# Mixture-of-experts stage of a four-layer graph network: units of 196 rows from a list made on the chip in place of 64 blocks of 784 rows

## The chip, the cores and the metric

The kernel runs on one core of a Trainium2 chip. The metric is the device time of one execution in microseconds (us). The kernel before has a median of 7043.7 us in 14 runs (7037.86 to 7055.6).

## The reference, cut to what matters

A graph of 12500 nodes with 128 features and 200000 edges goes through four layers, each followed by a residual and a layernorm: a weighted mean over neighbours, the layer below, and two more sums over neighbours. The change lies in the second layer: a graph convolution, then 64 experts of which every node uses two, then a batchnorm.

```python
new_feats = gcn_conv(feats, edge_src, edge_dst, W_conv, b_conv)
scores = new_feats @ gate_W + gate_b
topv, topi = top_k(scores, 2);  gw = softmax(topv)
# pos: how many earlier (node, choice) pairs took the same expert
C = 2 * ceil(2 * 12500 / 64)                     # 782
slot = eid * C + where(pos < C, pos, 0)
buf = zeros((64 * C, 128)).at[slot].add(where(pos < C, x_rep, 0))
hact = gelu(einsum('ecd,edh->ech', buf, W1) + b1)        # hidden width 256, exact gelu
y = einsum('ech,ehd->ecd', hact, W2) + b2
core = sum over the two choices of gw * y[slot] * (pos < C)
out = batchnorm(new_feats + core)
```

25000 pairs are spread over 64 experts, 391 on average, while 782 places are reserved for each.

## The kernel before

The engines are PE (TensorE; its loads of the stationary operand are listed as PEld), DVE (VectorE), ACT (ScalarE), POOL (GpSimd) and SP, which only issues transfers. SP, ACT and POOL each issue DMAs from an in-order queue of their own; an instruction that waits holds back all behind it on its engine. Around the change a scheduler orders the instructions of each engine from the program's order and the buffers that pools hold; nothing is placed by hand there. A pool with `bufs=2` lets the next loop step start before the last is done with its tile, and a tile in memory that an earlier stage held waits for that stage's last use.

The stages that matter, with line numbers of the profile:

- **First layer (to about 2140 us).** Edge messages are gathered and scattered by POOL (scatter at L751). Between, SP loads a window for each of 391 edge blocks, with a register load (L657) and a load at the register's address (L661). Among these loads stand the writes that fill `buf` with zeros: `buf` lies in DRAM with 64 x 784 rows for the experts and spare rows behind them for pairs without a place. Each write is 458 KB, one after every sixth window until 56 are done (L668 to L670).
- **Routing (3926 to 4235 us).** For groups of seven tiles of 128 nodes: convolution weights, scores, two maxima, softmax gates, and the place of each pair in its expert. `run` holds the number of pairs of each expert so far (L1363, L1364), `come` the row to fetch later (L1381). POOL scatters each tile's rows twice into `buf` (L1388).
- **Experts (4235 to 4823 us, L1398 to L1442).** `b1` is loaded and transposed once. The loop runs over 64 experts with SL = 784 rows each, as 7 tiles of TT = 112. Per expert SP loads `w1` (L1411) and `w2` (L1413), 128 KB each; ACT loads `b2` (L1415) and 392 KB of rows `xt` (L1417). PE transposes seven tiles (L1422), DVE copies them out (L1423, L1424). Four hidden groups follow, two halves of the hidden width by two halves of the rows: matmuls into 392 columns (L1429) and a gelu with `b1` on ACT (L1431). Then come 14 output products of 112 rows (L1436), one addition of `b2` on DVE (L1439), and a store of 392 KB into `ybuf` by SP (L1440). An f32 matmul of the program is several PE instructions in the trace: 256 hidden products are 512, 896 output products are 1792.
- **Counts.** Beside experts and combine the kernel makes tables for later edge sums: 98 counts (`band_counts`). One count is a set of comparisons on DVE (`fs` L1073, `fd` L1075), 17 PE instructions into four banks (L1089), four casts on ACT (L1091) and a store of 512 KB by SP (L1093). EXB = 48 of them are spread over the expert loop, the other 50 over the combine loop.
- **Combine (4823 to 5116 us).** For each of 98 node tiles and both choices POOL gathers 128 rows of `ybuf` (L1476) and DVE adds them with the gate (L1479); sums for the batchnorm follow every fourth tile.

The lines that set sizes and the fill:

```python
TT = 112
NTT = 7
SL = TT * NTT
DUMP = NE * SL
...
EXB = 48
...
                    if i % 6 == 5 and fill:
                        r = fill.pop(0)
                        Y.dma_start(bz[:, r:r + step], zero)
```

Of the kernel before, what the change touches and what calls it, by code (L numbers as in the profile page):

```python
# [10 lines left out]
F32 = mybir.dt.float32  # L11
# [3 lines left out]
I32 = mybir.dt.int32  # L15
AF = mybir.ActivationFunctionType
OP = mybir.AluOpType
AX = mybir.AxisListType
PSUM = bass.MemoryType.PSUM
DRAM = bass.MemoryType.DRAM  # L20

P = 128
N = 12500
D = 128
# [12 lines left out]
NE = 64  # L37
TOPK = 2
HID = 256
CAP = 2 * -(-N * TOPK // NE)  # L40
TT = 112
NTT = 7
SL = TT * NTT
DUMP = NE * SL
EPS = 1e-15
LN_EPS = 1e-5
# [18 lines left out]
LW = 96  # L65
WC = 16
BANK = 512
EXB = 48
MAXC = 256


# [67 lines left out]
def gnn_kernel(ctx: ExitStack, tc: tile.TileContext, a, out: bass.AP):  # L139
    nc = tc.nc  # L140
    V, S, G, T, Y = nc.vector, nc.scalar, nc.gpsimd, nc.tensor, nc.sync

    const = ctx.enter_context(tc.tile_pool(name="const", bufs=1))
    dram = ctx.enter_context(tc.tile_pool(name="dram", bufs=1, space=DRAM))
# [6 lines left out]
    iota = const.tile([P, P], F32, name="iota")  # L151
# [3 lines left out]
    ident = const.tile([P, P], F32, name="ident")  # L155
# [5 lines left out]
    ones = const.tile([P, P], F32, name="ones")  # L161
# [40 lines left out]
    off_d = [dram.tile([NK, P], I32, name=f"off_d{i}") for i in (0, 1)]  # L202
    counts = [dram.tile([NT, P, b.width], BF16, name=f"counts{i}") for i, b in enumerate(BANDS)]
    buf = dram.tile([DUMP + NT * TOPK * P, D], F32, name="buf")
    ybuf = dram.tile([DUMP, D], F32, name="ybuf")


    def newton_sqrt(pool, v, tag):
# [22 lines left out]
    def bc(v, n):  # L231
        return v[:, :, None].to_broadcast([P, v.shape[1], n])
# [256 lines left out]
    def spread_edges(bad):  # L489


        ET = mybir.EngineType
        NR = 6
        TAIL = NB - (NBK - 1) * P
        with tc.tile_pool(name="sc", bufs=1) as pc, tc.tile_pool(name="scp", bufs=1, space=PSUM) as pps:
            rows = pc.tile([P, NR, 4, W3], BF16, name="rows")
# [29 lines left out]
            if True:  # L526
# [3 lines left out]
                with tc.tile_pool(name="rf", bufs=1) as pa, tc.tile_pool(name="rfp", bufs=2, space=PSUM) as tp_:  # L530
# [105 lines left out]
            with tc.tile_pool(name="sb", bufs=4) as lp, tc.tile_pool(name="sw", bufs=3) as wk, \  # L636
                    tc.tile_pool(name="sg", bufs=2, space=PSUM) as gp:
                step = 7 * D
                zero = pc.tile([P, step], F32, name="zero")
                V.memset(zero, 0.0)  # L640
                bz = buf[0:DUMP, :].rearrange("(p r) f -> p (r f)", p=P)
                empty = list(range(NT - 1))
                fill = list(range(0, DUMP // P * D, step))
                one_ps = pps.tile([NT + 1, EB], F32, name="one_ps")
                V.memset(one_ps, 1.0)
                d_ps = pps.tile([P, NT], F32, name="d_ps")
                start = pc.tile([NT + 1, 1], F32, name="start")
# [3 lines left out]
                st = {"end": start}  # L651
                rb, win, hot, rank, low, gps = {}, {}, {}, {}, {}, {}

                def fetch(i):
                    rb[i] = lp.tile([P, 2 * EB], BF16, name="rb")
                    Y.dma_start(rb[i], rows_d[i].partition_broadcast(P))
                    _, at = nc.values_load_multi_w_load_instructions(  # L657
                        first_r[0:1, i:i + 1], engines=[ET.SP], min_val=0, max_val=NP - 1,
                        skip_runtime_bounds_check_because="clamped to the last node on the chip")
                    win[i] = lp.tile([P, 3, D + 1], BF16, name="win")  # L660
                    Y.dma_start(win[i].rearrange("p k f -> p (k f)"), table0[ds(at[0], P), :])  # L661
                    if 4 <= i < MID - 20 and empty:

                        for _ in range(-(-NT // (MID - 24))):
                            cl = clear(empty.pop(0), SURE, RB)
                            tc.declare_no_dep(cl.ins, group="spread", reason="rows that no edge has yet")
                            tc.add_to_no_dep_group("blank", cl.ins)
                    if i % 6 == 5 and fill:  # L668
                        r = fill.pop(0)
                        Y.dma_start(bz[:, r:r + step], zero)  # L670

                def places(i):
                    t = wk.tile([P, EB], BF16, name="hot")
# [36 lines left out]
                with tc.manual_schedule(engines={ET.DVE, ET.PE, ET.Activation}):  # L710
                    for i in range(-2, NB):
# [590 lines left out]
    with tc.tile_pool(name="moe", bufs=1) as pm:  # L1302
# [92 lines left out]
        at_.close()  # L1395


        with tc.tile_pool(name="ex", bufs=2) as wk, tc.tile_pool(name="exb", bufs=2, space=PSUM) as pb, \  # L1398
                tc.tile_pool(name="exh", bufs=2, space=PSUM) as ph_, tc.tile_pool(name="exc", bufs=1) as pc, \
                band_pools("x") as band:  # L1400
            b1n = pc.tile([NE, HID], F32, name="b1n")
            Y.dma_start(b1n, a["L1_gnn_b1"])
            b1T = pc.tile([P, 2, NE], F32, name="b1T")
            for j in range(2):
                pb1 = ph_.tile([P, 512], F32, name="ph")
                T.transpose(pb1[:, 0:NE], b1n[:, j * P:(j + 1) * P], ident[:NE, :NE])
                V.tensor_copy(b1T[:, j, :], pb1[:, 0:NE])
            HALF = SL // 2
            for e in range(NE):
                w1 = wk.tile([P, HID], F32, name="w1")  # L1410
                Y.dma_start(w1, a["L1_gnn_W1"][e])  # L1411
                w2 = wk.tile([P, 2, D], F32, name="w2")
                Y.dma_start(w2, a["L1_gnn_W2"][e].rearrange("(j p) d -> p j d", p=P))  # L1413
                b2 = wk.tile([TT, D], F32, name="b2")
                S.dma_start(b2, a["L1_gnn_b2"][e].partition_broadcast(TT))  # L1415
                xt = wk.tile([TT, NTT, D], F32, name="xt")
                S.dma_start(xt, buf[e * SL:(e + 1) * SL, :].rearrange("(i p) f -> p i f", p=TT))  # L1417
                px = pb.tile([P, 1024], F32, name="pw")
                bT = wk.tile([P, SL], F32, name="bT")
                for i in range(NTT):  # L1420
                    o = i * TT if i < 4 else 512 + (i - 4) * TT
                    T.transpose(px[:, o:o + TT], xt[:, i, :], ident[:TT, :TT])  # L1422
                V.tensor_copy(bT[:, 0:4 * TT], px[:, 0:4 * TT])  # L1423
                V.tensor_copy(bT[:, 4 * TT:SL], px[:, 512:512 + 3 * TT])  # L1424
                hT = wk.tile([P, 2, SL], F32, name="hT")
                for j in range(2):
                    for q in range(2):
                        ph = ph_.tile([P, 512], F32, name="ph")
                        T.matmul(ph[:, 0:HALF], w1[:, j * P:(j + 1) * P], bT[:, q * HALF:(q + 1) * HALF],  # L1429
                                 start=True, stop=True)  # L1430
                        S.activation(hT[:, j, q * HALF:(q + 1) * HALF], ph[:, 0:HALF], AF.Gelu,  # L1431
                                     bias=b1T[:, j, e:e + 1])
                py = pb.tile([P, 8, D], F32, name="pw")
                for i in range(NTT):
                    for j in range(2):
                        T.matmul(py[:TT, i, :], hT[:, j, i * TT:(i + 1) * TT], w2[:, j, :],  # L1436
                                 start=(j == 0), stop=(j == 1))
                ye = wk.tile([TT, NTT, D], F32, name="ye")
                V.tensor_tensor(ye, py[:TT, 0:NTT, :], b2[:, None, :].to_broadcast([TT, NTT, D]), OP.add)  # L1439
                Y.dma_start(ybuf[e * SL:(e + 1) * SL, :].rearrange("(i p) f -> p i f", p=TT), ye)  # L1440
                for s in range(EXB * e // NE, EXB * (e + 1) // NE):
                    band_counts(band, s)  # L1442


# [25 lines left out]
        with tc.tile_pool(name="cm", bufs=12) as wk, tc.tile_pool(name="cs", bufs=2) as sw, band_pools("c") as band:  # L1470
            for t in range(NT):
                for s in range(EXB + (NT - EXB) * t // NT, EXB + (NT - EXB) * (t + 1) // NT):
                    band_counts(band, s)
                for k in range(TOPK):
                    yk = wk.tile([P, D], F32, name="yk")
                    G.indirect_dma_start(out=yk, out_offset=None, in_=ybuf[:, :],  # L1476
                                         in_offset=bass.IndirectOffsetOnAxis(ap=come[:, t, k:k + 1], axis=0))
                    o = A3[:, t, 0:D]
                    V.scalar_tensor_tensor(o, yk, gates[:, t, k:k + 1], o, op0=OP.mult, op1=OP.add)  # L1479
                stats(sw, t)  # L1480
# [130 lines left out]
```

## Time and profile before

| what | value |
|---|---|
| median of 14 runs | 7043.7 us |
| profiled execution, its own time | 7042.59 us |
| its span in the trace | 7040.8 us |
| mean granted TensorE clock | 0.933 |
| instructions | 106434 |
| busy share of the span: PE, DVE, ACT, POOL | 73%, 61%, 29%, 55% |
| DMA | 1375.96 MB, mean 195 GB/s |
| routing, experts, combine | 309, 588, 293 us |

Times in the trace are microseconds from the start of the span. The span is 1.8 us shorter than the profiled execution's own time. A line of the timeline gives start, duration, engine, source line, operation, output and inputs by the program's names, and in brackets how long the engine had stood idle and what released it. A line of a group gives the number of instructions, the total busy time and the mean in nanoseconds of one, and the idle time before them with its releasers. The clock column is the share of full TensorE speed that was granted.

### The profile page before, as it was taken

Reading aid. Unit: us, or ns where it says so; the run is one execution under the profiler, and the core shown is the slowest. Engines: PE = TensorE matmul, PEld = TensorE weight load, DVE = VectorE, ACT = ScalarE, POOL = GpSimd, SP = SyncE. Lnnn points to the kernel's source line nnn. Section 1 sums busy time; section 2 is a strip of 40 time slices with the busy share of each in tenths; the row PEclk is TensorE's granted clock in tenths of the full one; section 3 lists DMA queues with packets and bytes.
Section 4 is the critical chain, followed back from the end, with each engine's and each line's share of the span. In section 5 each row is a group of like instructions: output and inputs, shape, how many; then the busy total and the mean of one; then the engine's idle time right before and its main releaser. Section 6 shows DMA issues by size and latency. Waiting matters only on the chain. (4 is left out here: it accounts for less than half of the span.)

```text
span 7040.8 us, 106434 instructions
## 1 busy us (share of the span) xinstructions
PE 5132.4 (73%) x32620; PEld 3139.8 (45%) x33009; DVE 4267.9 (61%) x11730; ACT 2018.9 (29%) x4176; POOL 3889.1 (55%) x3917
## 2 busy tenths in 40 slices
PE   0666666666664566699998548998809998699995
PEld 0444444444442233355554336664305444355544
DVE  6887777777775778766675574557991223411115
ACT  3343333333331223333332113444440001100003
POOL 0677777777773000577777570004707776477760
PEclk9999999999999888899999569999959999799998
DMA  9976555555557999355554115554458889688862
GB/s 247 272 220 204 159 152 153 152 152 151 151 153 231 324 318 303 124 165 165 166 166 151 47 56 159 166 164 137 142 156 277 288 291 294 205 293 290 282 230 63
DMA packets 1046137, 1375.96 MB, mean 195 GB/s; under 512 B 106732, under 2 KB 848744, under 8 KB 1045566
## 3 DMA queue, kind: packets, MB, share of 16 engines
q1 hardware_dynamic: 803208, 960.67, 44.4%
q0 software_dynamic: 181312, 376.38, 17.1%
q10 hardware_dynamic: 61046, 31.77, 1.6%
q8 instruction: 301, 4.93, 0.3%
q14 instruction: 270, 2.21, 0.1%
HBM read 911.40 MB, written 457.00 MB: 194 GB/s over the span
## 5 line engine op out<-in xcount | busy, mean ns | idle before, releaser
L1134 POOL DMA_INDIRECT fg<-table,e_row x1952 | 1956.9, 1003 | 1519.4 <-SPq L1023 676.8
L1125 PE MATMUL dense<-fc_a,fc_x 128*128 128x512 bf16 x7422 | 1874.8, 381 | 215.2 <-DMA fc_x<-table 205.3
L751 POOL DMA_INDIRECT msg<-rows,to x1564 | 1509.8, 965 | 656.8 <-issue 393.5
L1125 PEld LDWEIGHTS <-fc_x 128*128 128x128 bf16 x7644 | 678.5, 98 | 795.6 <-issue 194.6
L1227 DVE TENSOR_TENSOR AT<-AT,fps 128x512 f32 x122 | 83.9, 688 | 1490.4 <-PE fps L1151 1448.3
L1089 PE MATMUL fb_ps<-fd,fs 128*128 128x512 bf16 (+7 forms) x3942 | 877.1, 340 | 75.0 <-DMA fg<-table,e_row 31.5
L701 PE MATMUL g_ps<-rows,minus 128*128 128x258 bf16 x1564 | 462.7, 399 | 637.5 <-ACT rows L734 603.2
L734 ACT CAST rows<-g_ps 128x516 bf16<-128x516 f32 x1173 | 698.7, 596 | 642.0 <-PE g_ps L701 296.6
L695 PE MATMUL g_ps<-win,hot 128*128 128x129 bf16 x4692 | 650.6, 311 | 215.7 <-DMA win<-table 116.4
L1075 DVE TENSOR_SCALAR fd<-iota_h,hd 128x128 bf16<-128x128 f16 (+6 forms) x1563 | 786.6, 508 | 0.0
L1151 PEld LDWEIGHTS <-fg 128*128 128x128 bf16 x5856 | 464.1, 98 | 525.9 <-DMA fg<-table,e_row 97.9
L695 PEld LDWEIGHTS <-hot 128*128 128x128 bf16 x4692 | 535.3, 143 | 294.8 <-issue 195.2
L1151 PE MATMUL fps<-fh,fg 128*128 128x96 bf16 x5856 | 580.9, 208 | 95.8 <-DMA fg<-table,e_row 75.3
L868 PE MATMUL ce_sum<-ce_r,ce_s 128*128 128x390 bf16 x1764 | 380.5, 382 | 275.5 <-DVE ce_s L865 267.8
L1476 POOL DMA_INDIRECT yk<-ybuf,come x196 | 219.5, 1120 | 652.1 <-DMA counts<-bc_a 592.6
L1089 PEld LDWEIGHTS <-fs 128*128 128x128 bf16 x4108 | 377.1, 98 | 372.2 <-issue 110.0
L701 PEld LDWEIGHTS <-minus 128*128 128x128 bf16 x1564 | 199.7, 128 | 765.1 <-issue 765.0
L1091 ACT CAST fc_a<-fb_ps 128x512 bf16<-128x512 f32 x588 | 344.1, 585 | 634.0 <-PE fb_ps L1089 634.0
L679 DVE TENSOR_TENSOR_SCAN run_ps<-one_ps,run_ps,bin 99x512 f32<-99x512 f32 x390 | 505.4, 1296 | 13.8
L1073 DVE TENSOR_SCALAR fs<-iota_b,hs 128x128 bf16<-128x128 bf16 x1563 | 410.3, 265 | 39.4 <-PE fb_ps L1089 35.6
L868 PEld LDWEIGHTS <-ce_s 128*128 128x128 bf16 x1764 | 190.3, 112 | 465.8 <-DVE ce_s L865 259.6
L1091 ACT CAST bc_a<-fb_ps 128x512 bf16<-128x512 f32 x392 | 227.6, 584 | 448.5 <-PE fb_ps L1089 361.8
(382 smaller groups left out, 6245.3 us busy)
## 6 DMA issues: line engine op xcount, KB each, us to landing
ce_r<-msg SPq DMA_DIRECT2D x98, 1782.0 KB
fc_a<-counts SPq DMA_DIRECT2D x196, 768.0 KB
fc_a<-counts SPq DMA_DIRECT2D x196, 512.0 KB
rb<-rows_d SPq DMA_DIRECT2D x391, 256.0 KB
counts<-fc_a SPq DMA_DIRECT2D x98, 768.0 KB
counts<-bc_a SPq DMA_DIRECT2D x98, 512.0 KB
fc_x<-table SPq DMA_DIRECT2D x490, 96.0 KB
msg<-blank SPq DMA_DIRECT2D x99, 396.0 KB
```

The costliest lines, as they stand in the source:

```text
L679: V.tensor_tensor_scan(c, one_ps, b, st["end"], OP.mult, OP.add)
L695: T.matmul(gps[i][:, q, 0:D + 1], hot[i][:, q * P:(q + 1) * P], win[i][:, k, :], start=(q == 2 * half and k == 0), stop=False)
L701: T.matmul(gps[i][:, 2 * h:2 * h + 2, 0:D + 1], minus, r[:, 2 * h:2 * h + 2, k * W0:k * W0 + D + 1], start=False, stop=True, skip_group_ch ...
L734: S.copy(r[:, :, k * W0:k * W0 + D + 1], gt)
L751: sc = G.indirect_dma_start(out=msg[:, :], out_offset=bass.IndirectOffsetOnAxis(ap=to[:, q:q + 1], axis=0), in_=r[:, q, :], in_offset=None)
L868: T.matmul(ps, sel[:, j, :], r[:, j, 0:3 * W0], start=(j == 0), stop=(j == RB - 1))
L1075: V.tensor_scalar(col[:, 0:hi - lo], iota_h[:, 0:hi - lo], hd[self.i][:, s, q:q + 1], None, op0=OP.is_equal)
L1089: T.matmul(ps[:, lo - c0:hi - c0], self.sel[s, j], self.col[s, j][:, lo - w[j][0]:hi - w[j][0]], start=(j == first), stop=(j == js[-1]))
L1091: S.copy(out[:, c0:c1], ps)
L1125: T.matmul(dense[n], xr[s][:, k, :], cnt[s][:, n * BANK:(n + 1) * BANK], start=(s == 0 and k == 0), stop=(s == NT - 1 and k == 2))
L1134: G.indirect_dma_start(out=g[q][:, i].rearrange("p k f -> p (k f)"), out_offset=None, in_=table[:, :], in_offset=bass.IndirectOffsetOnAxis ...
L1151: T.matmul(ps[:, ds(at[0], LW)], g[i // 4][:, i % 4, k, :], hot[i // 4][:, i % 4, :], start=False, stop=(i == WC - 1 and k == 2))
```

## The change

Rows are computed in units of UR = 196 rows (two tiles of TT = 98), four units to an expert, so the place of each expert stays at 784 rows. A static loop runs over NU = 191 units, the most that 25000 pairs can need. Which expert and which rows a unit has is read from a list made on the chip: from the number of pairs of each expert, the number of units it needs, running sums of these, and for each unit the expert, the offset of its `b2`, the unit of rows to read and the unit of rows to write. The list goes through DRAM into one partition. Units past the last needed one read rows of the last expert and write to spare rows behind `ybuf`.

Each unit reads its entries into registers: two on SP, two on ACT, one on DVE. `w1`, `w2`, `xt` and the store use them as addresses, gelu's bias and the addition of `b2` as offsets. `b2` of all experts is loaded once, copied to 98 partitions. Weights are loaded for each unit, with three buffers in place of two. `ybuf`, parts of which are no longer written, is filled with zeros like `buf`, a write after every third window until 112 are done. EXB becomes 60, so 38 counts are left for the combine. The pools in PSUM have two buffers each for transposes, hidden and output tiles.

```diff
-TT = 112
-NTT = 7
-SL = TT * NTT
+TT = 98
+UR = 2 * TT
+UE = 4
+SL = UR * UE
+NU = (N * TOPK + NE * (UR - 1)) // UR
 DUMP = NE * SL
...
-EXB = 48
+EXB = 60
...
-    ybuf = dram.tile([DUMP, D], F32, name="ybuf")
+    ybuf = dram.tile([DUMP + NU * UR, D], F32, name="ybuf")
+    unit_d = dram.tile([8, P], I32, name="unit_d")
...
-                    if i % 6 == 5 and fill:
-                        r = fill.pop(0)
-                        Y.dma_start(bz[:, r:r + step], zero)
+                    if i % 3 == 2 and fill:
+                        Y.dma_start(fill.pop(0), zero)
...
+            b2r = pc.tile([TT, NE * D], F32, name="b2r")
+            Y.dma_start(b2r, a["L1_gnn_b2"].rearrange("e d -> (e d)").partition_broadcast(TT))
             b1n = pc.tile([NE, HID], F32, name="b1n")
             Y.dma_start(b1n, a["L1_gnn_b1"])
...
+                T.matmul(t_ps[:, 0, 0:NE], ones, run, start=True, stop=True)
+                n = pu.tile([P, NE], F32, name="un_n")
+                V.tensor_scalar_min(n, t_ps[:, 0, 0:NE], float(CAP))
+                u = pu.tile([P, NE], F32, name="un_u")
+                V.tensor_scalar(u, n, 0.0, None, op0=OP.is_gt)
+                for k in range(1, UE):
+                    V.scalar_tensor_tensor(u, n, float(k * UR), u, op0=OP.is_gt, op1=OP.add)
+                end = pu.tile([P, NE], F32, name="un_end")
+                V.tensor_tensor_scan(end, ones[:, 0:NE], u, 0.0, OP.mult, OP.add)
...
+                T.transpose(w_ps[0:8, 0, 0:P], what.rearrange("p w k -> p (w k)"), ident)
+                w_i = pu.tile([8, P], I32, name="un_i")
+                V.tensor_copy(w_i, w_ps[0:8, 0, 0:P])
+                Y.dma_start(unit_d, w_i)
+                Y.dma_start(unit_r, unit_d.rearrange("w p -> (w p)").rearrange("(o c) -> o c", o=1))
...
+            def number(kind, j, engine, most):
+                _, v = nc.values_load_multi_w_load_instructions(
+                    unit_r[0:1, kind * 2 * P + j:kind * 2 * P + j + 1], engines=[engine], min_val=0, max_val=most,
...
+                return v[0]
...
-            for e in range(NE):
+            for j in range(NU):
+                e = number(0, j, ET.SP, NE - 1)
+                w1 = wk.tile([P, 1, HID], F32, name="w1")
+                Y.dma_start(w1, w1s[:, ds(e, 1), :])
+                w2 = wk.tile([P, 1, 2, D], F32, name="w2")
+                Y.dma_start(w2, w2s[:, ds(e, 1), :, :])
+                xt = wk.tile([TT, 1, 2, D], F32, name="xt")
+                S.dma_start(xt, rows_in[:, ds(number(2, j, ET.Activation, NE * UE - 1), 1), :, :])
+                px = pb.tile([P, UR], F32, name="px")
+                for i in range(2):
+                    T.transpose(px[:, i * TT:(i + 1) * TT], xt[:, 0, i, :], ident[:TT, :TT])
+                bT = wk.tile([P, UR], F32, name="bT")
+                V.tensor_copy(bT, px)
+                ph = pb.tile([P, 2, UR], F32, name="ph")
+                hT = wk.tile([P, 2, UR], F32, name="hT")
+                e1 = number(0, j, ET.Activation, NE - 1)
+                for k in range(2):
+                    T.matmul(ph[:, k, :], w1[:, 0, k * P:(k + 1) * P], bT, start=True, stop=True)
+                    S.activation(hT[:, k, :], ph[:, k, :], AF.Gelu, bias=b1T[:, k, ds(e1, 1)])
+                py = pb.tile([P, 2, D], F32, name="py")
+                for i in range(2):
+                    for k in range(2):
+                        T.matmul(py[:TT, i, :], hT[:, k, i * TT:(i + 1) * TT], w2[:, 0, k, :],
+                                 start=(k == 0), stop=(k == 1))
+                ye = wk.tile([TT, 1, 2, D], F32, name="ye")
+                e2 = number(1, j, ET.DVE, (NE - 1) * D)
+                for i in range(2):
+                    V.tensor_tensor(ye[:, 0, i, :], py[:TT, i, :], b2r[:, ds(e2, D)], OP.add)
+                st = Y.dma_start(rows_out[:, ds(number(3, j, ET.SP, NE * UE + NU - 1), 1), :, :], ye)
...
+                for s in range(EXB * j // NU, EXB * (j + 1) // NU):
                     band_counts(band, s)
...
-                    G.indirect_dma_start(out=yk, out_offset=None, in_=ybuf[:, :],
+                    G.indirect_dma_start(out=yk, out_offset=None, in_=ybuf[0:DUMP, :],
```

More of the change, by code (lines that the diff above doesn't have):

```diff
@@ L640, in spread_edges @@
                 V.memset(zero, 0.0)
-                bz = buf[0:DUMP, :].rearrange("(p r) f -> p (r f)", p=P)
+                blanks = [b[0:DUMP, :].rearrange("(p r) f -> p (r f)", p=P) for b in (buf, ybuf)]
                 empty = list(range(NT - 1))
-                fill = list(range(0, DUMP // P * D, step))
+                fill = [b[:, r:r + step] for b in blanks for r in range(0, DUMP // P * D, step)]
                 one_ps = pps.tile([NT + 1, EB], F32, name="one_ps")
@@ L1395, in gnn_kernel @@
         at_.close()
-        with tc.tile_pool(name="ex", bufs=2) as wk, tc.tile_pool(name="exb", bufs=2, space=PSUM) as pb, \
-                tc.tile_pool(name="exh", bufs=2, space=PSUM) as ph_, tc.tile_pool(name="exc", bufs=1) as pc, \
-                band_pools("x") as band:
+        ET = mybir.EngineType
+        with tc.tile_pool(name="ex", bufs=3) as wk, tc.tile_pool(name="exp", bufs=2, space=PSUM) as pb, \
+                tc.tile_pool(name="exc", bufs=1) as pc, band_pools("x") as band:
+            unit_r = pc.tile([1, 8 * P], I32, name="unit_r")
+            b1T = pc.tile([P, 2, NE], F32, name="b1T")
+            b2r = pc.tile([TT, NE * D], F32, name="b2r")
+            Y.dma_start(b2r, a["L1_gnn_b2"].rearrange("e d -> (e d)").partition_broadcast(TT))
@@ L1401, in gnn_kernel @@
             b1n = pc.tile([NE, HID], F32, name="b1n")
             Y.dma_start(b1n, a["L1_gnn_b1"])
-            b1T = pc.tile([P, 2, NE], F32, name="b1T")
             for j in range(2):
[L1405 to L1408, printed above, removed]
-            for e in range(NE):
[L1410 to L1441, printed above, removed]
@@ new lines, in gnn_kernel @@
+                pb1 = pb.tile([P, 2, UR], F32, name="ph")
+                T.transpose(pb1[:, 0, 0:NE], b1n[:, j * P:(j + 1) * P], ident[:NE, :NE])
+                V.tensor_copy(b1T[:, j, :], pb1[:, 0, 0:NE])
+            with tc.tile_pool(name="un", bufs=1) as pu:
+                t_ps = pb.tile([P, 2, UR], F32, name="ph")
+                T.matmul(t_ps[:, 0, 0:NE], ones, run, start=True, stop=True)
[7 more added lines that the diff above has]
+                V.tensor_tensor_scan(end, ones[:, 0:NE], u, 0.0, OP.mult, OP.add)
+                shift = pu.tile([P, NE], F32, name="un_shift")
+                V.tensor_sub(shift, u, end)
+                V.scalar_tensor_tensor(shift, iota[:, 0:NE], float(UE), shift, op0=OP.mult, op1=OP.add)
+                ji = pu.tile([P, 2], I32, name="un_ji")
+                G.iota(ji, pattern=[[P, 2]], base=0, channel_multiplier=1)
+                jf = pu.tile([P, 2], F32, name="un_j")
+                V.tensor_copy(jf, ji)
+                pick = pu.tile([P, 2, NE], F32, name="un_pick")
+                V.tensor_tensor(pick, end[:, None, :].to_broadcast([P, 2, NE]), bc(jf, NE), OP.is_le)
+                what = pu.tile([P, 4, 2], F32, name="un_what")
+                V.tensor_reduce(what[:, 0, :], pick, AX.X, OP.add)
+                V.tensor_scalar_min(what[:, 0, :], what[:, 0, :], float(NE - 1))
+                V.tensor_scalar_mul(what[:, 1, :], what[:, 0, :], float(D))
+                V.tensor_tensor(pick, iota[:, None, 0:NE].to_broadcast([P, 2, NE]), bc(what[:, 0, :], NE), OP.is_equal)
+                V.tensor_tensor(pick, pick, shift[:, None, :].to_broadcast([P, 2, NE]), OP.mult)
+                V.tensor_reduce(what[:, 2, :], pick, AX.X, OP.add)
+                V.tensor_add(what[:, 2, :], what[:, 2, :], jf)
+                V.tensor_scalar_min(what[:, 2, :], what[:, 2, :], float(NE * UE - 1))
+                over = pu.tile([P, 2], F32, name="un_over")
+                V.tensor_tensor(over, jf, end[:, NE - 1:NE].to_broadcast([P, 2]), OP.is_ge)
+                V.tensor_scalar_add(what[:, 3, :], jf, float(NE * UE))
+                V.tensor_sub(what[:, 3, :], what[:, 3, :], what[:, 2, :])
+                V.tensor_mul(what[:, 3, :], what[:, 3, :], over)
+                V.tensor_add(what[:, 3, :], what[:, 3, :], what[:, 2, :])
+                w_ps = pb.tile([P, 2, UR], F32, name="ph")
+                T.transpose(w_ps[0:8, 0, 0:P], what.rearrange("p w k -> p (w k)"), ident)
[3 more added lines that the diff above has]
+                Y.dma_start(unit_r, unit_d.rearrange("w p -> (w p)").rearrange("(o c) -> o c", o=1))
@@ new lines, in number @@
+            def number(kind, j, engine, most):
+                _, v = nc.values_load_multi_w_load_instructions(
+                    unit_r[0:1, kind * 2 * P + j:kind * 2 * P + j + 1], engines=[engine], min_val=0, max_val=most,
+                    skip_runtime_bounds_check_because="clamped to the last expert's units on the chip")
+                return v[0]
+            rows_in = buf[0:DUMP, :].rearrange("(u i p) f -> p u i f", i=2, p=TT)
+            rows_out = ybuf.rearrange("(u i p) f -> p u i f", i=2, p=TT)
@@ new lines, in gnn_kernel @@
+            w1s = a["L1_gnn_W1"].rearrange("e p h -> p e h")
+            w2s = a["L1_gnn_W2"].rearrange("e (j p) d -> p e j d", p=P)
+            for j in range(NU):
[27 more added lines that the diff above has]
+                st = Y.dma_start(rows_out[:, ds(number(3, j, ET.SP, NE * UE + NU - 1), 1), :, :], ye)
+                if j:
+                    tc.declare_no_dep(st.ins, group="units", reason="each unit has rows of its own")
+                tc.add_to_no_dep_group("units", st.ins)
+                for s in range(EXB * j // NU, EXB * (j + 1) // NU):
```

## The prediction

> **What bounds the kernel now.** I read the page's busy slices and its chain first: the chain that ended last puts 3% on the matmul line L1436, 3% on L1429 and 1% on L1422, so the experts' matmuls lie on the path. Then I cut the span into stages with the windows view (columns: busy time and instructions of PE, PEld, DVE, ACT and POOL; granted clock; DMA share; GB/s). The rows are routing, experts, combine.
>
> ```profile
> 3926.00:4235.00 309.00, 163.48 (x640) 106.06 (x640) 218.63 (x837) 48.74 (x68) 200.03 (x198) 0.61 0.14 46
> 4235.00:4823.00 588.00, 577.39 (x3449) 407.24 (x3513) 293.56 (x706) 250.44 (x437) 0.00 (x0) 0.99 0.56 163
> 4823.00:5116.00 293.00, 240.83 (x935) 96.76 (x953) 262.68 (x825) 131.91 (x228) 219.49 (x196) 0.97 0.40 135
> ```
>
> In the expert stage PE is busy 577 of 588 us at clock 0.99: TensorE bounds it, and every matmul taken out pays. In the combine stage no engine is full, but POOL's gathers come one behind another. The timeline shows the stage's two ends: the last routing scatter, the first transpose, the first gather.
>
> ```profile
> 4232.48 0.96 POOL L1388 DMA_INDIRECT buf<-ACC,goi  x1 [0.30 <-issue]
> ...
> 4241.75 1.54 PE L1422 MATMUL pw<-ident,xt 112*128 112x112 f32 x7 [35.91 <-DMA xt<-buf]
> ...
> 4826.06 1.34 POOL L1476 DMA_INDIRECT yk<-ybuf,come  x1 [592.62 <-DMA counts<-bc_a]
> ```
>
> So PE stands still 35.9 us until the first rows land at 4241.75, and the gathers wait for the last store; what the stage gains or loses, the first gather shows. One expert on PE, from its timeline (start, duration; a busy group ends in a modelled tail, so I use start to start):
>
> ```profile
> 4290.05 3.27 PE L1436 MATMUL pw<-w,hT 128*112 128x128 f32 x28
> ...
> 4293.16 0.84 PE L1422 MATMUL pw<-ident,xt 112*128 112x112 f32 x7
> ...
> 4293.83 1.38 PE L1089 MATMUL fb_ps<-fd,fs 128*128 128x320 bf16 x5
> ...
> 4295.05 1.57 PE L1429 MATMUL ph<-bT,w 128*128 128x392 f32 x4
> ...
> 4296.46 0.65 PE L1089 MATMUL fb_ps<-fd,fs 128*128 128x448 bf16 x3
> ...
> 4296.94 1.51 PE L1429 MATMUL ph<-bT,w 128*128 128x392 f32 x4
> ```
>
> That is 3.11 us for 28 output matmuls (0.111 each), 0.67 for 7 transposes (0.096 each), 1.41 and 1.35 for two groups of 4 hidden matmuls (0.345 each): 6.54 per expert. Count matmuls go at 0.212 and one count has 17: 3.6 us. 48 counts belong to the stage, 3 were made during routing: 64 x 6.54 + 45 x 3.6 = 581, against 577 measured. The model holds, and I use it for the change.
>
> **1. Units (gain).** A unit has 2 transposes of 98 (0.084 each, scaled by columns), 4 hidden matmuls of 196 columns (half of 0.345) and 8 output matmuls: 0.17 + 0.69 + 0.89 = 1.75 us. The static loop runs all 191 units, however few the tokens fill: 334 us for 419 before, **-85**.
>
> **2. More counts in the stage (loss).** 60 for 48. While PE waits at the start more is made ahead; by the instruction order some 8 counts precede the first unit, so 52 remain: 52 x 3.6 = 187 for 162, **+25**. Units and counts together are 521.
>
> **3. The start (loss).** The b2 table (3.2 MB), the b1 load, the list and all register loads lie in memory that routing held, so they wait for the last scatter. It landed at 4235.3, when the first row load was issued. The 3.2 MB are priced by GB/s of the page's slices: 324 gives 10 us, 219 gives 15; I take 11. b1 lands behind it on SP's queue at about 4248.5. Then come PE transposes, some 23 small DVE operations (about 0.22 us each) and the 7 pairs of count comparisons (0.63) between them on DVE: 9.5 us, to 4258.5. Transpose and copy 1.5, two small transfers at 2.45 (the landing of a 64 KB gather or a count store), a register load, issue and landing of the rows: first transpose at about 4269 for 4241.75, **+27** (bounds 4262 to 4285). The one POOL operation of the list stands among the scatters and delays none. Nothing hides the start but the counts already in point 2.
>
> **4. Register loads and addresses.** Five loads per unit. The trace has them on SP and on DVE (minimum/median/maximum ns):
>
> ```profile
> L657 SPq TENSOR_LOAD <-first_r x391: 262/271/1078, 186.4 to 2130.3; - x196
> L1223 DVEq TENSOR_LOAD <-l_base x122: 299/305/1251, 2889.0 to 6833.4; - x122
> ```
>
> With them, per unit: SP two loads, three issues at 0.33 to 0.43 and a third of a count's store, about 2.0 us; DVE 0.35 for the copy, 0.57 for the adds, 0.3 for the load and 1.03 for comparisons, about 2.2; ACT, which loses the b2 load of each expert, about 1.5. All are under PE's 2.8 (1.75 and 0.3 counts), so by themselves 0.
>
> The Trainium skill speaks against this ("DMA: Bandwidth & Descriptors", section "Latency and other measured facts"): a register load has a floor of about 600 ns, against the 271 and 305 here. By its figure, an estimate, SP would hold 2.7 us a unit and the loop in point 5 would grow to about 2.8; the sum would end some 5 us higher. I go by the rows.
>
> **5. New wait (loss).** In SP's queue the store of unit j stands ahead of the weight loads of unit j+3, and with three buffers those refill what unit j used. So: hidden matmul 0.35, gelu wait 0.5, transposes 0.17, last outputs 0.33, adds 0.67, store issue 0.33, register load and address 0.34, and the landing L must fit in two units: period (2.7 + L)/2. L: three times the row load on ACT follows when an earlier weight load, issued on SP, has landed: 4394.85 to 4396.46, 4403.75 to 4406.31, 4451.06 to 4453.39, mean 2.2 us. Period 2.45, under 2.8 where counts lie between, over 1.75 in the first 17 units, which by the order have hardly any: 17 x 0.7 = 12. At some later units the load stands one store further back; 6 for them: **+18** (bounds 0, if L is hidden, to +60, rival A).
>
> **6. End (0) and combine.** From the last output's end, 4820.7, to the first gather are 5.4 us; the smaller last unit gives about 5. First gather: 4269 + 521 + 18 + 5 = 4813 for 4826, **-13**. 12 counts leave the combine:
>
> ```profile
> L1476 POOL DMA_INDIRECT yk<-ybuf,come x196 | 219.5, 1120 | 652.1 <-DMA counts<-bc_a 592.6 <-DVE fs L1073 20.1 <-DMA yk<-ybuf,come 18.3
> ```
>
> 196 x (1.12 + 0.30 of issue) = 279 us, the length of the stage, so POOL's issue binds it, and PE's saved 43 us are worth nothing there. The scatter in routing takes 0.955 where DVE idles; (1.12 - 0.955) x 196 over 50 counts is 0.66 us a count: **-8** (bounds -5 to -32, if all stretching went).
>
> **7. Second zero fill.** 56 more writes of 458 KB among the edge gathers. POOL's scatter rate in that stage is 1.265 us at 198 GB/s and 1.27 at 152: the transfers lie beside POOL. **0** (to +5 where the DMA share nears 1).
>
> **Sum:** -13 - 8 = -21 against the profiled execution's 7042.59 us: **7022**. That execution is 1.1 us under the median of 7043.7, well inside the runs' spread. Steps 1, 2, 3, 5 and the end are what make the -13: -85 + 25 + 27 + 18 leaves -15, rounding and end the rest.
>
> **Rivals.** The break-even is where the unit stage takes 21 us more, 560 us: 2.93 us a unit.
>
> A, slower: the weight loop of point 5 becomes the bound everywhere. DMA share rises, weights are read 191 times instead of 64. For it: the stage already has 0.56, and 25 MB of weights more come; feature loads of 96 KB took 4.4 to 8.7 us where the share was about 0.88. Against it: the row loads and stores shrink with the rows, and a 512 KB count store landed in 2.45. It decides from L = 3.2 us; at 3.5 the period is 3.1, the stage 592 and the time about **7075**.
>
> The same section of the skill gives HBM's access latency as 0.2 us on average and 2 us at high load; no row here separates it. By it, as an estimate, L could reach 4.0 and the time some 7120.
>
> B, same: gelus and casts in order on ACT, copies and comparisons in order on DVE make PE wait a little in every unit, so the period is 2.9. For it: in before, PE's loads of the stationary operand for L1429 already waited 95 times for a gelu, 37.4 us in all (the waits view), and a unit of half the columns leaves less to cover that; against it, PE has counts to put between. 554 us: about **7037**.
>
> C, faster: the weight loop is hidden and the start reaches 4262; the first gather comes at 4788, and the combine sheds 8 to 32: **6996 to 6973**.
>
> D: the change doesn't shorten what it says, since 191 units are computed whatever the tokens fill; that is in point 1 already. If 3.2 MB land slowest, point 3 is +43 and the time 7038, as in B.
>
> **Chances.** Within 0.2% (14 us) is about what a measurement of this kernel can tell from no change. Forecast (7005 to 7028) 0.33, C 0.17, B and D 0.21, A 0.29: faster 0.50, same 0.21, slower 0.29. The range must reach into A and C: 6985 to 7080 leaves out C's end (0.06) and A's long tail (0.13).
>
> **What would show it.** First transpose near 4269; 191 units at 2.8 us with PE busy above 0.9 of the stage; first gather near 4813 and gathers of mean 1.08; register loads near 0.3 on all three engines. Wrong: PE idle before the hidden matmuls with a weight load as the releaser (A) or a gelu (B); a first transpose past 4285; units near 2.5 with counts (C).

## The result, and the profile after

The change made the kernel slower: 7130.8 us median in 6 runs (7122.14 to 7135.37), against 7043.96 in 28 runs of the kernel before. The ratio is 1.0121 (95% interval 1.0111 to 1.0131). The profiled execution took 7141.4 us, its span 7139.6. The predicted 7022 and the range up to 7080 were both too low.

The windows view of the kernel after, cut at the last scatter of routing, the first row transpose and the first gather (the columns are those of the prediction):

```profile
3979.00:4240.10 261.10, 137.51 (x522) 89.29 (x523) 196.84 (x775) 41.67 (x61) 201.48 (x196) 0.61 0.16 53
4240.10:4276.00 35.90, 15.28 (x64) 7.17 (x65) 13.72 (x54) 8.11 (x14) 0.96 (x1) 0.67 0.54 184
4276.00:4925.80 649.80, 571.63 (x3501) 425.06 (x3559) 358.35 (x1193) 273.44 (x593) 0.01 (x1) 0.98 0.59 180
4925.80:5204.00 278.20, 203.06 (x709) 79.74 (x723) 213.45 (x660) 98.60 (x170) 218.76 (x196) 0.90 0.34 114
```

The third row is the loss: 650 us from first transpose to first gather, where before has 584 and the sum had 544. PE is busy 572 of 650, so it waits now; in before it was full. Combine is as long as before (278), the start takes 36 us for 9. The timeline shows the start's steps:

```profile
4240.12 0.96 POOL L1390 DMA_INDIRECT buf<-ACC,goi  x1 [0.30 <-issue]
4242.65 0.38 SPq L1406 DMA_DIRECT2D b2r<-in_L_gnn_b  x1
...
4257.43 0.44 PE L1411 MATMUL ph<-ident,b1n 64*128 64x64 f32 x2 [40.63 <-DMA b1n<-in_L_gnn_b]
...
4267.69 0.24 SPq L1454 DMA_DIRECT2D unit_r<-unit_d  x1
...
4276.10 0.39 PE L1477 MATMUL px<-ident,xt 98*128 98x98 f32 x2 [2.81 <-DMA xt<-buf]
...
4925.79 1.32 POOL L1534 DMA_INDIRECT yk<-ybuf,come  x1 [684.71 <-DVE fs L1075]
```

What PE waited for in the loop, from the waits view (us in total, times, longest):

```profile
PEld ph L1484 <- ACT hT L1485: 86.9, 133, 2.2
PE ph L1484 <- ACT hT L1485: 36.1, 69, 1.7
PEld py L1489 <- ACT hT L1485: 31.0, 93, 1.0
PEld ph L1484 <- DMA w<-in_L_gnn_W: 24.1, 39, 1.9
PE ph L1484 <- DMA w<-in_L_gnn_W: 15.6, 23, 1.5
...
ACT hT L1485 <- DMA xt<-buf: 60.0, 59, 3.0
```

Both suspects of the prediction are there: gelus (B) and weight loads (A). The last row gives one reason why gelus are late: 59 times ACT had just issued a row load. The chain of waits through the same loop is on PE for only 63%; in before it is on PE for 99% (the first line is before, the second after):

```profile
by line: PE pw L1436 34.1%; PE ph L1429 32.6%; PE fb_ps L1089 24.4%; PE pw L1422 7.9%; issue 0.7%; DMA counts<-bc_a 0.4%; ACT hT L1431 0.1%; ACT bc_a L1091 0.1%; ACTq L1431 0.0%
```

```profile
by line: PE ph L1484 21.4%; PE py L1489 20.6%; PE fb_ps L1091 17.7%; DMA w<-in_L_gnn_W 8.7%; ACT hT L1485 7.7%; issue 4.6%; ACTq L1458 4.3%; PE px L1477 3.7%; DMA xt<-buf 3.2%; ACT bc_a L1093 2.8%; ACTq L1474 2.1%; SPq L1458 1.0%; ACTq L148
```

What the register loads and the row load's issue cost on their queues (ns, minimum/median/maximum):

```profile
L1458 SPq TENSOR_LOAD <-unit_r x382: 262/457/1037, 4271.3 to 4918.9; - x191
L1458 ACTq TENSOR_LOAD <-unit_r x382: 273/452/1314, 4272.1 to 4915.9; - x191
L1458 DVEq TENSOR_LOAD <-unit_r x191: 298/306/1145, 4280.5 to 4918.1; - x191
...
L1474 ACTq DMA_DIRECT2D xt<-buf x191: 565/567/663, 4273.2 to 4891.7; - x191
```

### The profile page after: what moved, and what is told of

It reads as the page before. It is cut to its first block, busy times and chain, and to the rows that moved or that the text cites. A ratio compares the mean times of both kernels' runs of the same rounds, so it can differ in the third digit from the quotient of the medians.

```text
span 7139.6 us, 111414 instructions
## 1 busy us (share of the span) xinstructions
PE 5121.6 (72%) x32555; PEld 3159.5 (44%) x32934; DVE 4305.7 (60%) x12135; ACT 2025.5 (28%) x4302; POOL 3898.7 (55%) x3918
## 5 line engine op out<-in xcount | busy, mean ns | idle before, releaser
L1091 PE MATMUL fb_ps<-fd,fs 128*128 128x512 bf16 (+7 forms) x3951 | 903.6, 344 | 99.5 <-DVE fd L1077 71.3
L1534 POOL DMA_INDIRECT yk<-ybuf,come x196 | 219.7, 1121 | 744.1 <-DVE fs L1075 702.1
```

The source lines that it names most:

```text
L1091: T.matmul(ps[:, lo - c0:hi - c0], self.sel[s, j], self.col[s, j][:, lo - w[j][0]:hi - w[j][0]], start=(j == first), stop=(j == js[-1]))
```

## The experiments

Every kernel below is the changed kernel with the edit shown. "Start" is from the last scatter to the first transpose, "loop" from there to the first gather; their sum is compared where an edit moves work from one to the other. In the sets e1 to e4 and e13 to e16 all kernels, the kernel before too, took some 15% longer (before 8117 and 8137 us, in the other sets 7048 to 7052), some 460 us of it in the first layer; ratios are within a set. Loops agree across sets to a few us: 547 in e8, 545 in e15, which is e8 with one load more.

| run | edit | start | loop | sum | combine | ratio to before (95%) |
|---|---|---|---|---|---|---|
| before | | 9 | 584 | 594 | 277 | 1 |
| after | | 36 | 650 | 686 | 278 | 1.0121 (1.0111 to 1.0131) |
| e1 | no bias register | 36 | 638 | 674 | 303 | 1.0105 (1.0075 to 1.0134) |
| e2 | six buffers | 6 | 670 | 676 | 299 | 1.0110 (1.0071 to 1.0148) |
| e3 | rows by POOL | 41 | 633 | 674 | 298 | 1.0109 (1.0079 to 1.0138) |
| e4 | fixed addresses | 18 | 559 | 578 | 287 | 0.9986 (0.9964 to 1.0008) |
| e5 | none | 35 | 649 | 684 | 279 | 1.0132 (1.0102 to 1.0161) |
| e6 | stores by POOL | 36 | 702 | 737 | 278 | 1.0196 (1.0166 to 1.0225) |
| e7 | rows and stores by POOL | 35 | 589 | 624 | 276 | 1.0026 (1.0014 to 1.0038) |
| e8 | e7, six buffers, 48 counts | 6 | 547 | 553 | 274 | 0.9937 (0.9915 to 0.9960) |
| e9 | (order on SP) | 36 | 725 | 761 | 278 | 1.0231 (1.0201 to 1.0261) |
| e10 | (order on ACT) | 37 | 653 | 690 | 278 | 1.0125 (1.0096 to 1.0154) |
| e11 | 48 counts | 36 | 631 | 667 | 277 | 1.0097 (1.0068 to 1.0126) |
| e12 | e7, six buffers | 7 | 591 | 597 | 274 | 0.9999 (0.9988 to 1.0011) |
| e13 | one more load on SP | 36 | 744 | 780 | 298 | 1.0210 (1.0189 to 1.0230) |
| e14 | one more load on ACT | 37 | 671 | 708 | 302 | 1.0125 (1.0095 to 1.0156) |
| e15 | e8, one more load on SP | 12 | 545 | 557 | 304 | 0.9976 (0.9952 to 1.0000) |
| e16 | e8, 44 counts | 12 | 535 | 548 | 294 | 0.9966 (0.9946 to 0.9985) |
| e17 | six buffers, weights early | 5 | 645 | 650 | 279 | 1.0078 (1.0058 to 1.0098) |
| e18 | e17, rows by POOL | 7 | 600 | 606 | 280 | 1.0018 (1.0008 to 1.0027) |

### First set: one suspect at a time

e1:

```diff
-                e1 = number(0, j, ET.Activation, NE - 1)
-                    S.activation(hT[:, k, :], ph[:, k, :], AF.Gelu, bias=b1T[:, k, ds(e1, 1)])
+                    S.activation(hT[:, k, :], ph[:, k, :], AF.Gelu, bias=b1T[:, k, 0:1])
```

> The changed kernel with one of ACT's two register loads per unit taken out: gelu takes the bias of expert 0 in every unit (the output is then not the reference's). Measured from the first row transpose to the first gather, 650 us in the changed kernel. If ACT's in-order queue sets the loop (the theory now: two register loads of 0.45 us and a row-load issue of 0.57 stand between the gelus), the stage loses 40 to 86 us (191 x 0.45 at most). If the weight loads behind the stores set it (rival A of the prediction), it stays within 10 us. If it is the sum of short waits in each unit whatever their engine, it loses 10 to 40.

Loop 638: 12 us less. This is the range named for a sum of short waits.

e2:

```diff
-        with tc.tile_pool(name="ex", bufs=3) as wk,
+        with tc.tile_pool(name="ex", bufs=6) as wk,
```

> The changed kernel with six buffers in place of three for weights, rows and results, so that the weight loads can be issued up to three units earlier. If weight loads set the loop (rival A), the 650 us fall towards the 544 of the prediction, by 60 us or more. If ACT's queue sets it, less than 20 us. The waits of PE for a weight load, 40 us in all, should vanish in both cases.

The fall of 60 did not come: the loop grew by 20, the sum fell by 10. And PE still waited for weights (34 us before the hidden matmuls, for 40). The start fell to 6 us: the larger pools put b2's table, b1 and the list elsewhere, and they no longer wait for routing. Three counts that were made in that start fall into the loop; at 3.6 us each they would be 11 us of the loop's growth, the rest is open.

e3:

```diff
-                S.dma_start(xt, rows_in[:, ds(number(2, j, ET.Activation, NE * UE - 1), 1), :, :])
+                G.dma_start(xt, rows_in[:, ds(number(2, j, ET.Pool, NE * UE - 1), 1), :, :])
```

> The changed kernel with the row loads (register load and issue) on POOL's queue, which is idle in this stage, in place of ACT's. If ACT's queue sets the loop, 0.45 + 0.57 + 0.1 us leave it in each unit and the 650 us fall by 80 to 110. If weight loads set it, within 10 us. A row load that POOL issues may land later than one of ACT; with three buffers that is two units ahead.

17 us less in the loop and 12 in the sum, far from 80. PE's waits for weight loads grew from 40 to 71 us: with gelus earlier, weights are late.

e4, the list's code left out as well:

```diff
-                e = number(0, j, ET.SP, NE - 1)
+                e, r = j // 3, j // 3 * UE + j % 3
```

> The list and all register loads left out: 191 units with addresses known when the program is built, three for each expert (two for the last), so that rows past the 588th of an expert are not computed. The work in matmuls, gelus, copies, additions, weights, rows and counts is that of the changed kernel. If register loads and address arithmetic are what the loop lost, the 650 us fall to 540 to 570. If weight loads set it, SP's part of the chain shortens by some 0.5 us in two units: 600. If units of this size have too many short waits in themselves, it stays above 620. The start should come 12 to 15 us earlier, since the list and its two trips through memory are gone and b2 and b1 still wait for the last scatter.

559 us: the work itself, with 191 loads of weights, fits in that. The run drops only what reading the addresses brought, and the order that came with it: its weight loads are also issued earlier (fifth set), so it does not part register loads from late weights.

### Second set: both queues

e5 and e6:

```diff
-                st = Y.dma_start(rows_out[:, ds(number(3, j, ET.SP, NE * UE + NU - 1), 1), :, :], ye)
+                st = G.dma_start(rows_out[:, ds(number(3, j, ET.Pool, NE * UE + NU - 1), 1), :, :], ye)
```

> The changed kernel itself, for a stage length on the chip that the other runs of this set use. First transpose to first gather 650 us as in its first profile, within 15.

> The changed kernel with the stores of the results (register load and issue) on POOL's idle queue in place of SP's. The theory now: SP's queue is full. In the middle of the loop its loads, issues, address arithmetic and the fixed gaps between them fill 3.05 of 3.34 us a unit. Without the store it has about 1.9, so the stage falls from 650 to 570 to 600, and ACT's queue or PE is next. Against it: if the loop is a chain of short waits in which SP is only one, the stage falls by less than 30, as it did when the row load left ACT. If the weight loads were late because they stand behind stores that wait, and not because SP is full, the stage falls as well, but the gaps in SP's queue were then waits; in the first profile they were 46 of 500 us.

e5 repeats 649. e6 went the other way: 702. Weight loads are no longer late (0.4 us of PE's waits), but gelus are, more than before:

```profile
ACT hT L1485 <- DMA xt<-buf: 160.3, 108, 3.6
PEld ph L1484 <- ACT hT L1485: 129.7, 97, 2.9
...
PE ph L1484 <- ACT hT L1485: 92.8, 59, 2.6
```

So a full SP queue was not the cause by itself. The scheduler also put ACT's row loads elsewhere in its order: 27 times two in a row ahead of a gelu (about 3 us of loads and issues), for 2 times in the changed kernel.

e7 joins the edits of e3 and e6; e8 adds six buffers and EXB = 48.

> Row loads and stores both on POOL's queue: SP keeps one register load and the weight loads, ACT one register load, gelus and casts. By the theory that SP is full first and ACT next, PE is the bound again: 540 to 565, near the 559 with fixed addresses. POOL then has about 2.4 us a unit. By the chain of short waits: above 600.

> As before it, with six buffers and 48 counts in the stage. Six buffers also moved the b2 table, b1 and the list to memory that routing doesn't hold: from last scatter to first transpose 6 us for 36. 12 counts fewer take 43 us of PE out of the stage, and 12 more in the combine cost nothing by the two profiles (277 and 278 us). Start and loop together: 6 + 510 to 530, about 60 under the kernel before, so the time is 40 to 60 below that of before on the same chip. If counts do stretch the gathers, the combine is 8 us longer.

Alone the two edits gave -17 and +53 in the loop, together -60: each queue hid the other. e7's 589 lies between the two expectations; 68 us over the 521 of matmuls remain. e8 is faster than both kernels, 0.9937, some 48 us under before as expected, though its start and loop, 553, are above the 516 to 536 of the text. Its loop and combine:

```profile
4247.00:4794.00 547.00, 517.05 (x3356) 401.51 (x3406) 321.32 (x1091) 253.77 (x556) 276.17 (x379) 0.99 0.68 205
4794.00:5069.00 275.00, 231.50 (x897) 92.34 (x916) 254.63 (x798) 125.02 (x216) 215.36 (x196) 0.98 0.42 139
```

### Third set: an added load, and the counts

e9 adds the call `number(0, j, ET.SP, NE - 1)`, e10 `number(0, j, ET.Activation, NE - 1)`; e11 is EXB = 48; e12 is e8 with 60 counts.

> The changed kernel with one more register load per unit on SP, whose value isn't used. If SP's queue is full (its instructions and fixed gaps fill 91% of the loop), the stage grows by what SP has no slack for: 0.47 + 0.05 less 0.3 of waits a unit, 40 to 100 us on 649. If ACT's queue alone sets the loop, it grows by less than 15. The scheduler may put other work in another order; a change of 15 us can come from that alone.

> The changed kernel with one more register load per unit on ACT, ahead of the gelus, whose value isn't used. If the waits of PE for gelus come from what stands ahead of them in ACT's queue, each unit's first gelu comes 0.46 us later: the stage grows by 40 to 88 us. If SP alone sets the loop, less than 15.

The added loads are not in the programs that ran: both traces have 382 register loads on SP, 382 on ACT and 191 on DVE, as e5. The two runs test something else: the same loads, transfers and matmuls in another order (e9 also has one more semaphore instruction of 17 ns per unit on SP). e9 took 725, that is 76 us for order all but alone. e10 kept its length (653) with another weakness: its weights are issued 7.5 us ahead (median), its rows only 3.05, and row loads make up 20.8% of its chain.

> The changed kernel with 48 counts in the stage in place of 60, so 50 in the combine. By the prediction's sum the 12 counts cost 43 us of PE here and save 8 in the combine. If the two queues set the loop, the counts fill PE's idle time and only their casts and stores (4 x 0.58 on ACT, 0.4 on SP per count) count: the stage falls by 10 to 25. The combine is 277 to 280 us long, as with 38 counts.

18 us less, so 12 counts cost 1.5 us each here: most of their 3.6 us of PE lay in time in which PE waited.

> Row loads and stores on POOL, six buffers, 60 counts: it tells the buffers from the counts in the faster version. From last scatter to first transpose 6 us. The 12 counts go to PE, which is near its bound there: stage 547 + 43 = 590 if PE is full, 547 + 20 if a third of PE's time was idle. Start and loop 575 to 596, so 7030 to 7050.

Loop 591, time 7045.6, ratio 0.9999: the units, laid out this way, just reach the kernel before. From e12 to e8 the 12 counts are worth 44 us, the full 3.7 each.

### Fourth set: the price of a load

e13 gives `w2` a register load of its own on SP, e14 the second gelu one on ACT, e15 is e13's edit in e8, e16 is e8 with EXB = 44.

> The changed kernel with a register load of its own for the second weight load of each unit: three loads on SP per unit, all used. SP's recorded instructions and the usual gaps between them fill 91% of the loop. If a full SP queue sets the loop, the stage grows from 649 by 40 to 90 us; if order or ACT does, by less than 20.

> The changed kernel with a register load of its own for the second gelu of each unit: three loads on ACT per unit, all used. If gelus late behind register loads set the loop, the stage grows by 40 to 88 us; if SP does, by less than 20.

e13 took 744 us and e14 671; 95 more is just past the first range, 22 more lies between the two of e14. e9 and e10 are nearest to them in order (weight loads behind the store of two units before: 92 of 150 in e13, 93 in e9). Against their 725 and 653 the loads themselves cost at most 19 and 18 us, 0.1 us a unit (e13's second weight loads stand a little later still than e9's). Against e5 e13 is +95; without e9 that would have been read as SP's full queue.

> The faster version (rows and stores on POOL, six buffers, 48 counts; stage 547 us) with the same added load on SP. There SP is filled to 70%, so the load should find room: less than 12 us more. If it costs 40 us or more here too, a full queue is not the cause, but the lateness of the weight load itself.

> The faster version with 44 counts in the stage and 54 in the combine. Each count moved out saved (591 - 547) / 12 = 3.7 us of the stage, so 15 us for four. DVE is busy some 250 of 277 us in the combine with 50 counts and needs 3.8 us a count, so four more fill it: the combine stays within 5 us. Some 12 us under the faster version's 7004.

e15 costs nothing, as expected. e16's loop is 10 us under e15's, where 15 were expected; 54 counts do not lengthen the combine (294 against 304 in the same set), and the ratios of the two runs overlap.

### Fifth set: only the place of the weight loads

Counting the stores that SP issued ahead of each unit's first weight load (`w1`), in units 30 to 179: in the changed kernel 106 of 150 stand behind the store of three units before, as the prediction had it, and 43 behind that of two units before. In e2 it is 109 and 39, in e9 57 and 93. The second load (`w2`) stands behind the store of two units before 80 times in the changed kernel. In e4 all stand behind the store of four or five units before. (The text on record for e17 counts one unit too few.) The median time from a weight load's issue to the unit's first hidden matmul is 3.05 us in the changed kernel.

```diff
-            for j in range(NU):
-                e = number(0, j, ET.SP, NE - 1)
+            ahead = {}
+            for j in range(-3, NU):
+                if j + 3 < NU:
+                    e = number(0, j + 3, ET.SP, NE - 1)
...
+                    ahead[j + 3] = w1, w2
+                if j < 0:
+                    continue
+                w1, w2 = ahead.pop(j)
```

> The changed kernel with six buffers, as in e2, and with the weight loads of a unit issued three units ahead: all of them then stand behind the store of three units before, where it was two or one. SP's instructions are the same in number and kind. If the place of the weight loads behind the stores sets the loop, the stage falls from e2's 670 by 60 us or more, and the time from a weight load's issue to the unit's first hidden matmul grows from 3.2 to over 5 us. If SP's queue is full, the stage stays above 640. If ACT's row loads then set it, as they did when the stores left SP, it stays near 700.

> As e17, and the row loads on POOL: neither weights nor gelus are late, with register loads, stores and weight loads all left on SP. By the theory of order the stage is as long as with both row loads and stores on POOL and six buffers, 591, within 15. If SP's load counts as well (3.05 us a unit, 583 in all), 600 to 640.

In both all 150 loads stand behind the store of four units before. e17: 650 for e2's 676 in start and loop, and 5.8 us from issue to use. The loop's 645 falls by 25 and not by 60; taken by itself it fits the text's "above 640" for a full SP, which e18 then contradicts. Weights are hardly waited for now (6.5 us); gelus are:

```profile
PEld ph L1490 <- ACT hT L1491: 78.3, 122, 2.7
ACT hT L1491 <- DMA xt<-buf: 75.0, 54, 3.2
...
PEld py L1495 <- ACT hT L1491: 57.3, 104, 2.1
...
PE ph L1490 <- ACT hT L1491: 36.1, 63, 2.2
```

e18: 606, with a loop of 600. That lies in both of its ranges (576 to 606 by order, 600 to 640 if SP's load counts), so it does not part them. The long waits for gelus are gone, the short ones stay (longest 0.9 and 0.5 us), and weights are waited for a little again:

```profile
PEld ph L1490 <- ACT hT L1491: 60.1, 151, 0.9
...
PEld py L1495 <- ACT hT L1491: 46.9, 134, 0.5
...
PEld ph L1490 <- DMA w<-in_L_gnn_W: 15.5, 20, 2.2
```

SP is full here: its instructions and the usual gap after each kind fill 295 of 300 us in the middle of the loop (91% in the changed kernel). Against e12, which has the stores on POOL and the weight loads in the changed kernel's place, the sum is only 9 us longer.

## Why the prediction was wrong, point by point

**1, units, and 2, counts: right in size.** Nothing measured speaks against 521 us of PE work: back to back, matmuls start 169 ns apart (hidden), 109 (output) and 88 (transposes) in e12, as assumed; e4 runs the units and 4.5 counts more in a loop of 559, e8 with 43 us less in 547, and a count is worth 3.7 us where PE is the bound (e12 to e8). 7.8 counts were made ahead of the first unit, for the 8 assumed. In the changed kernel PE isn't the bound, and there a count is worth 1.5.

**3, the start: right.** 36 us for 9, +27 as worked out; b1's transposes came at 4257.4, the list's store to the first row load at the predicted distance, all later by the 7.6 us by which routing ended later. The reason given, memory that routing held, is borne out by e2: other places, 6 us.

**4, register loads: the step that failed first.** It said of SP, ACT and DVE "All are under PE's 2.8 (1.75 and 0.3 counts), so by themselves 0". The busy time per unit was too small: SP has 3.05 us of 3.34 a unit in the middle of the loop, not 2.0, since loads take 0.465 on average for 0.271, and address arithmetic and the gaps between instructions come to some 0.8. But SP, filled to 295 of 300 us in e18, is worth only 9 us there. What the step left out is the order in the queue: register loads (0.45) and a row issue of 0.57, where a fixed address took 0.33, stand ahead of gelus that PE waits for. PE waited for 226 of the 382 gelus of the changed kernel; 115 of these began over 0.15 us after their hidden matmul had ended, 71 us in all, and ACT spent 35 us of that in register loads and 10 in the instructions of row loads. In e18 one gelu that PE waited for is late in this way, in before none. Moving the row load and its register load to POOL, with weights early, took 44 us off (e17 to e18).

The Trainium skill ("DMA: Bandwidth & Descriptors", section "Latency and other measured facts") gives a register load a floor of about 600 ns. It was right that the row of 271 was too low for this loop; the floor itself isn't seen here, with medians of 457, 452 and 306 and a minimum of 262. In e7, with rows and stores on POOL, SP's median is 274 and ACT's 283; what sets the longer ones was not tried.

**5, the new wait: mis-sized.** The mechanism and rival A's place are right: weight loads behind stores. "At some later units the load stands one store further back; 6 for them" was 43 of 150 units (80 for `w2`); one store earlier for all took 26 us off (e2 to e17). L was right: the 23 weight pieces of the chain through the loop have a median of 2.25 us, for an assumed 2.2 and a break-even at 3.2. The weights were late because of where they stood, not because the DMA queues were slower. (Rival A's 25 MB of weights more should read 33: 127 more units of 256 KB.)

By the same section's HBM latency of 2 us at high load L would have been up to 4.0, as an estimate; the longest of those 23 pieces is 3.33, at a DMA share of 0.59.

**Rival B: mis-sized.** It was priced at 2.9 us a unit, 15 us over the forecast. With both queues relieved (e12) start and loop are 597, some 58 us over the 539 that 6.5 of start, 334 of units and 55 counts (198) would give. That is 0.3 us a unit, 5 us of the whole being the end. The size of the unit is not enough to explain it: e4 has the same units and fixed addresses, and its loop of 559 is 22 us over the same sum (334 and 56.5 counts, 203), where e12's 591 is 59 over (334 and 198). In e12 59 gelus that PE waited for are still late, 48 us in all, 29 of it in ACT's register loads. The rest was not taken apart.

**6, combine: wrong in its small term.** 38 and 50 counts leave the gathers as long as they were, with the same mean (1121 ns here, 1120 before, 1117 in e11); 54 have 1180 for e15's 1165, 3 us in all:

```profile
L1534 POOL DMA_INDIRECT yk<-ybuf,come x196 | 219.7, 1121 | 744.1 <-DVE fs L1075 702.1
```

So POOL's issue does bind the combine, as step 6 said, but the 0.165 us over the routing scatter does not come from the counts: 8 us of the error.

**7, second fill: right.** Routing's scatters began 4.2 us later in the profiled run, 2.9 in e5, and 3.9 us earlier than before in e12, all three with the fill. Routing itself took 3.5 us longer; in all 7.6 us, not foreseen.

Together: 105 us in the loop, 8 in the combine, 8 ahead of it make up the 119 between the forecast's span and the measured one (the rest is rounding). Walking from the changed kernel to the faster one in start and loop (e2 is from a slower set, whose sums can differ by some 5 us): 686, other places 676 (e2), weights one store earlier 650 (e17), rows off ACT 606 (e18), stores off SP 597 (e12), 12 counts back to the combine 553 (e8). e17 and e18 are steps of order and queue alone, and the scheduler's order can shift with every one of these steps; what the 76 us of e9 are made of beside the weights' place was not tried.

## What to carry to other kernels

When a big step is cut into small ones, price the queue of every engine in order, not its busy time: write down for each wait what stands ahead of it, and how many steps ahead a load is really issued. More buffers don't move a load that the order keeps behind a store; in e2 six buffers changed nothing of it. Relieve two queues together before one of them is ruled out: here one alone gave 17 us, the other cost 53, both gave 60.

## What the runs showed that was not expected

All but the same instructions in another order took 76 us more of 649 (e9). An edit that seems to add one load must be read against a run of its order.

The clock column of the first layer shows 1.00 in before and 0.50 in after, with matmuls there as long as they were (windows view of the same 250 us of both, then the group of each page). The first two lines are before, the two others are after:

```profile
1250.00:1500.00 250.00, 152.68 (x1178) 119.02 (x1178) 195.56 (x491) 98.05 (x197) 190.25 (x197) 1.00 0.51 152
...
L695 PE MATMUL g_ps<-win,hot 128*128 128x129 bf16 x4692 | 650.6, 311 | 215.7 <-DMA win<-table 116.4
```

```profile
1250.00:1500.00 250.00, 151.67 (x1176) 118.49 (x1176) 195.67 (x490) 97.92 (x196) 190.22 (x197) 0.50 0.52 151
...
L697 PE MATMUL g_ps<-win,hot 128*128 128x129 bf16 x4692 | 650.7, 311 | 206.9 <-DMA win<-table 110.6
```

In groups of several the 129-column matmuls start 108 ns apart in both (median), so the two columns are not two speeds. The profile of before holds no clock record ahead of 2202 us, and 1.00 is what the column shows where there is none; that of after holds one from 86 us on, 2123 us long. Which of the two values was the true clock is not shown. Runs of the changed kernel with a mean clock of 0.78 took 7122 to 7141 us, those with 0.93 took 7130 to 7134, so a mean clock of 0.78 in place of 0.93 is no sign of a slower run here.
